# A recurrent step's tail re-ordered: which logarithm goes first on ScalarE, and where the 1e-10 term stands on VectorE

## The chip, the cores and the metric

The kernel runs on one core of a Trainium2 chip. The metric is the device time of one execution in microseconds; lower is better. The time of the kernel before is the median of three runs.

## What is computed

The reference is a network of eight sublayers on an input of 2 x 2048 x 256. The change lies in the first sublayer only, a recurrence over the 2048 positions ("the scan"). Its state h is a complex number for each of 2 batches, 256 channels and 16 modes. Cut to what matters, one position does this:

```
def step(h, inp):
    x_t, dt_t, B_t, C_t, xr_t = inp
    h_carrier = h.mean(axis=1)                        # over the 256 channels
    T = cos((c_phase(xr_t) - c_phase(h_carrier)) / 2) ** 2
    alpha = exp(dt_t[..., None] * A_neg)
    expo = 1 + (1 - alpha) * 0.5 * (1 - T[:, None, :])
    mag, ph = c_mag(h), c_phase(h)                    # c_mag = sqrt(re^2 + im^2 + 1e-8)
    cmag = minimum(exp(expo * log(mag + 1e-8)), 10)   # c_phase = arctan2(im, re + 1e-10)
    h = from_polar(cmag, ph) + B_t * (dt_t * x_t)
    h = from_polar(tanh(c_mag(h)), c_phase(h))
    y_t = einsum('bnc,bdnc->bd', C_t, h)
    return h, y_t
```

So each position needs the one before it: a power of the magnitude, an added drive, then a tanh of the new magnitude at unchanged phase.

## The kernel before

Before the scan, `scan_tables` computes the tables that it reads and puts them into DRAM. After it come an output product and the other seven sublayers. The scan keeps the state on 128 partitions (2 batches x 16 modes x 4 groups of channels) with 64 channels in the free dimension, real and imaginary part apart, so nearly every operation of a step is one instruction on a 128 x 64 tile of fp32.

The loop over the positions has four rounds of 512 positions. Inside a round everything is written out: 32 groups of 16 positions, and within a group `step(k, ...)` for each position. Inside a round the program keeps the order in which the instructions are written (`tc.manual_schedule()`), each engine working through its own queue in that order; semaphore waits are derived from the data. Where an instruction has to wait for two engines, an event-semaphore instruction for the first wait stands ahead of it.

A step uses three engines, in this order of data:

- TensorE (line 407) turns the sums of the last state, `hs`, into the mean over the channels, `hc` and `hd`. ScalarE makes the inverse of its magnitude out of it (`sq` on line 415, `ln`, `ci`), VectorE a product with the normalised input (`dot`).
- VectorE multiplies the carried logarithm `lg` by the decay (`gl`, line 411), subtracts it from the carried `kd` (`ex`, line 421) and makes `ngd` from `gl` and `dot` (line 422). ScalarE makes the two factors `ea` (line 426) and `fac` (line 436) with Exp. VectorE multiplies the state by them and adds the drive `bx` (lines 433 to 441): `p`, the new state before the tanh.
- VectorE squares and adds: `m2` (line 448), the squared magnitude, and `r1` (line 450).
- The tail: ScalarE makes out of `m2` and `r1`, in a run of Ln and Exp, all that the tanh and the next step's logarithm need. `lm` is log m2, `m` the magnitude, `ir` the inverse of the radius, `e` = exp(-2m), `rm` the inverse of m^2, `le` = log(1 + e), `ld` = log(1 - e), `sg` = 1/(1 + e), `lb` = log(m2 + 1e-8), `k1` and `k2c` two small corrections. tanh m is (1 - e) sg.
- VectorE scales `p` by `ir` (line 472) and by e - 1 (line 474). Line 477 makes `dl`, the correction for the 1e-10 of the phase. Line 479 multiplies by `sg`, writes the new state into `hist` and its sum over the 64 channels into `hs`; each of the two is a custom instruction with a read of the accumulator behind it. Lines 483 to 486 make `th` = ld - le, `kc`, and from them the `lg` and `kd` of the next step.

`lm`, `m` and `lr` are tiles in PSUM (`le` reuses the tile `m`, `lb` the tile `lr`), each in a pool with one buffer for each name; the others lie in SBUF with two buffers each. In between, `act_gap` gives ScalarE the next step's drive and some work for the next group, and `dve_gap` gives VectorE a little work in some steps.

Of the kernel before, what the change touches and what calls it, by code (L numbers as in the profile page):

```python
# [17 lines left out]
AF = mybir.ActivationFunctionType  # L18
ALU = mybir.AluOpType
# [18 lines left out]
SMALL = 1e-10  # L38
MAG_EPS = 1e-8
# [20 lines left out]
def new(pool, shape, name, **kw):  # L60
    return pool.tile(list(shape), F32, name=name, tag=name, **kw)


class Kernel:
# [189 lines left out]
    def scan(self, y, dtd, dxd, tabd):  # L254
# [7 lines left out]
        V, A, G = nc.vector, nc.scalar, nc.gpsimd  # L262
        J, TURN = 64, TG * GROUPS
        with ExitStack() as c:
# [129 lines left out]
            w = lambda sh, name: new(wp, [P, *sh], name)  # L394
            wa = lambda name: new(pa, [P, J], name)

            def step(k, g, before, act_gap, dve_gap):

                tc_, ng, dx, cs = tg[g]
                ng = ng[:, k]  # L400
                h = hist[g][:, k - 1] if k else hist[1 - g][:, TG - 1]
                hn = hist[g][:, k]
                i, o = (k + 1) % 2, k % 2

                for out in (hc, hd):
                    for r in range(0, P, 32):
                        nc.tensor.matmul(out[r : r + 32], mean[:, r : r + 32], hs[i], start=True, stop=True)  # L407
                before()

                gl, ex, ea, ngd = (w([J], n) for n in ("gl", "ex", "ea", "ngd"))  # L410
                V.tensor_tensor(gl, lg[i], ng, ALU.mult)


                sq, n2c = w([2], "sq"), w([1], "n2c")
                A.activation(sq, hc, AF.Square, accum_out=n2c)  # L415
                junk, dot = w([2], "junk"), w([1], "dot")
                V.tensor_tensor_reduce(
                    out=junk, in0=hd, in1=tc_[:, 4:6, k], scale=1.0, scalar=0.0, op0=ALU.mult, op1=ALU.add,
                    accum_out=dot,
                )  # L420
                V.tensor_tensor(ex, kd[i], gl, ALU.subtract)  # L421
                V.tensor_scalar(ngd, gl, dot, None, ALU.mult)
                ln, ci = wa("lr")[:, 0:1], w([1], "ci")
                A.activation(ln, n2c, AF.Ln, bias=1e-18)
                A.activation(ci, ln, AF.Exp, scale=-0.5)  # L425
                A.activation(ea, ex, AF.Exp)  # L426


                nc.tensor.matmul(hd[32:33, 0:1], ci, self.ident[:, 0:1], start=True, stop=True)  # L429


                p = w([2, J], "p")
                V.scalar_tensor_tensor(p[:, 0], h[:, 0], SMALL, ea, ALU.add, ALU.mult)  # L433
                V.tensor_tensor(p[:, 1], h[:, 1], ea, ALU.mult)  # L434
                fac = w([J], "fac")
                A.activation(fac, ngd, AF.Exp, scale=ci)  # L436
                act_gap(k)
                for k2 in range(2):
                    V.tensor_tensor(p[:, k2], p[:, k2], fac, ALU.mult)  # L439
                for k2 in range(2):  # L440
                    V.tensor_tensor(p[:, k2], p[:, k2], bx[o][:, k2], ALU.add)  # L441
                z = w([J], "z")
                V.scalar_tensor_tensor(z, p[:, 0], -2.0 * SMALL, p[:, 0], ALU.add, ALU.mult)
                q = w([2, J], "q")
                V.tensor_tensor(q[:, 1], p[:, 1], p[:, 1], ALU.mult)
                V.tensor_tensor(q[:, 0], p[:, 0], p[:, 0], ALU.mult)
                m2 = w([J], "m2")
                V.scalar_tensor_tensor(m2, z, MAG_EPS, q[:, 1], ALU.add, ALU.add)  # L448
                r1 = w([J], "r1")
                V.scalar_tensor_tensor(r1, q[:, 0], 1e-19, q[:, 1], ALU.max, ALU.add)  # L450
                dve_gap(k)

                lm, m, lr = wa("lm"), wa("m"), wa("lr")
                A.activation(lm, m2, AF.Ln)  # L456
                A.activation(lr, r1, AF.Ln)
                A.activation(m, lm, AF.Exp, scale=0.5)
                ir, e, sg, rm, ld = (w([J], n) for n in ("ir", "e", "sg", "rm", "ld"))
                A.activation(ir, lr, AF.Exp, scale=-0.5)  # L460
                A.activation(e, m, AF.Exp, scale=-2.0)
                A.activation(rm, lm, AF.Exp, scale=-1.0)
                le = wa("m")
                A.activation(le, e, AF.Ln, bias=1.0)
                A.activation(ld, e, AF.Ln, scale=-1.0, bias=1.0)
                A.activation(sg, le, AF.Exp, scale=-1.0)  # L466
                lb, k1, k2c = wa("lr"), w([J], "k1"), w([J], "k2c")
                A.activation(lb, m2, AF.Ln, bias=MAG_EPS)
                A.activation(k1, rm, AF.Ln, scale=MAG_EPS, bias=1.0)
                A.activation(k2c, lb, AF.Exp, scale=-0.5)  # L470
                for k2 in range(2):
                    V.tensor_tensor(p[:, k2], p[:, k2], ir, ALU.mult)  # L472
                for k2 in range(2):
                    V.scalar_tensor_tensor(p[:, k2], e, -1.0, p[:, k2], ALU.add, ALU.mult)  # L474
                th, kc, dl = (w([J], n) for n in ("th", "kc", "dl"))

                V.scalar_tensor_tensor(dl, p[:, 0], 0.5 * SMALL, rm, ALU.mult, ALU.mult)
                for k2 in range(2):
                    V.tensor_tensor_reduce(  # L479
                        out=hn[:, k2], in0=p[:, k2], in1=sg, scale=-1.0, scalar=0.0 if k2 else J * SMALL,  # L480
                        op0=ALU.mult, op1=ALU.add, accum_out=hs[o][:, k2 : k2 + 1],
                    )
                V.tensor_tensor(th, ld, le, ALU.subtract)
                V.scalar_tensor_tensor(kc, k2c, 2.0 * MAG_EPS, k1, ALU.mult, ALU.add)
                V.scalar_tensor_tensor(lg[o], th, 2.0, kc, ALU.mult, ALU.add)
                V.scalar_tensor_tensor(kd[o], kc, 0.5, dl, ALU.mult, ALU.add)

# [23 lines left out]
            with tc.For_i(0, S, TURN) as iv:  # L511
                A.preload_act_table_set(LOG_EXP)
                with tc.manual_schedule():
                    late = None
                    for g in range(GROUPS):
# [4 lines left out]
                        def act_gap(k):  # L520
                            for k2 in range(2):
                                if k + 1 < TG:
                                    drive(j, k + 1, k2, (k + 1) % 2)
                                else:
                                    drive(nxt, 0, k2, 0)
                            if k == 1:
                                rows(iv + (g + 1) * TG, nxt)
                            if 3 <= k < 11:
                                decay(nxt, (k - 3) // 2 * 4, 4, (k - 3) % 2)

                        def dve_gap(k):
                            if k == 1 and late is not None:
                                outputs(*late)
                            if k in (3, 4):
                                picked(nxt, k - 3)

                        for k in range(TG):
                            def before():
                                if k:
                                    project(j, k - 1, yps)  # L540
                                elif late is not None:
                                    project(1 - j, TG - 1, late[1])

                            step(k, j, before, act_gap, dve_gap)
# [1151 lines left out]
```

## Time and profile before

| | us |
|---|---|
| median of 3 runs | 14359.62 (14356.21 to 14366.0) |
| the profiled execution, its own time | 14346.1 |
| its span | 14344.4 |
| span up to the first step, 0 to 365 | 365 |
| the scan, 365 to 10164 | 9799; VectorE busy 8279, ScalarE 7244, TensorE 2275 |
| all that follows, 10164 to 14344.4 | 4180; VectorE busy 1789, ScalarE 1176, TensorE 3382 |

The scan takes two thirds of the span. In it none of the engines is busy all the time. An instruction's time in the profile is a start and a duration; two instructions of one engine can overlap in it, because the next starts before the end of the one ahead is reported. Times in the timeline count from the start of the span.

### The profile page before, as it was taken

The page shows a single profiled execution, that of the slowest core. Times are in us where ns is not written, and L with a number is a line of the kernel's source. Part 1 is how long each engine was busy: PE and PEld are TensorE (multiplying, and loading weights), DVE is VectorE, ACT ScalarE, POOL GpSimd, SP SyncE. Part 2 cuts the span into 40 slices and gives each one's busy share as a digit, 9 for nine tenths or more (in the row PEclk, how much of TensorE's full clock was granted, in tenths as well). Part 3 has the DMA queues.
Part 4 walks back from the last instruction along what each step waited for, and adds up shares of the span by engine and source line. Part 5 has one row for each costly group of instructions (what it writes and reads, how often), then busy time and mean ns, then how long its engine had stood idle before and what let it go on. Part 6 is the DMA issues. An engine that isn't in the chain of part 4 may idle for free. (4 is left out here: it accounts for less than half of the span.)

```text
span 14344.4 us, 281730 instructions
## 1 busy us (share of the span) xinstructions
PE 5813.5 (41%) x76520; PEld 3906.4 (27%) x76520; DVE 10318.8 (72%) x65163; ACT 8541.6 (60%) x44786; POOL 419.1 (3%) x496
## 2 busy tenths in 40 slices
PE   4222222222222222222222222222698566978889
PEld 2111111111111111111111111111355444544445
DVE  6888888888888888888888888888576211455552
ACT  3777777777777777777777777777354000134442
POOL 0000000000000000000000000000000000121110
PEclk6555555555555555555555555555598788989999
DMA  3000000000000000000000000000000777132210
GB/s 78 13 16 15 15 16 16 14 16 16 14 16 16 13 17 16 13 16 16 13 16 17 13 16 16 16 14 16 13 4 21 170 182 173 40 77 35 34 28 14
DMA packets 349084, 461.07 MB, mean 32 GB/s; under 512 B 204930, under 2 KB 244937, under 8 KB 346452
## 3 DMA queue, kind: packets, MB, share of 16 engines
q1 hardware_dynamic: 296276, 319.90, 9.9%
q10 hardware_dynamic: 36352, 88.61, 2.6%
q0 software_dynamic: 14848, 34.36, 0.9%
q8 instruction: 612, 10.03, 0.3%
q14 instruction: 996, 8.16, 0.2%
HBM read 385.55 MB, written 52.46 MB: 31 GB/s over the span
## 5 line engine op out<-in xcount | busy, mean ns | idle before, releaser
L407 PE MATMUL hc<-hs,mean 128*32 128x2 f32 x16384 | 586.9, 203 | 7227.7 <-DVE hs L479 7164.0
L407 PEld LDWEIGHTS hc<-hs,mean 128*32 128x32 f32 x16384 | 411.1, 140 | 7441.1 <-DVE hs L479 7376.8
L472 DVE TENSOR_TENSOR p<-p,ir 128x64 f32<-128x64 f32 x4096 | 738.2, 221 | 1064.6 <-ACT ir L460 1064.6
L491 PE MATMUL yps<-cs,hist 128*64 128x8 f32 x8192 | 1225.0, 259 | 13.3 <-DVE hs L479 13.3
L456 ACT ACTIVATE lm<-m 128x64 f32<-128x64 f32 x2048 | 466.2, 228 | 1209.8 <-DVE m L448 1209.8
L388 ACT ACTIVATE bx<-dx,tc 128x64 f32<-128x64 f32 x4098 | 1169.5, 332 | 0.1
L1520 ACT ACTIVATE d_p<-ps_e 128x512 f32<-128x512 f32 (+3 forms) x1280 | 599.5, 537 | 757.5 <-PE ps_o L1501 532.0
L491 PEld LDWEIGHTS yps<-cs,hist 128*64 128x64 f32 x8192 | 1033.2, 218 | 45.4 <-DVE hs L479 13.8
L415 ACT ACTIVATE sq<-hc 128x2 f32<-128x2 f32 x2048 | 352.6, 172 | 1162.5 <-PE hc L407 1162.5
L479 DVE CUSTOM_DVE_ANT_0 hist<-p,sg 128x64 f32<-128x64 f32 x4096 | 746.6, 219 | 11.9 <-DVE hs L479 6.1
L474 DVE SCALAR_TENSOR_TENSOR p<-e,p 128x64 f32<-128x64 f32 x4096 | 738.3, 222 | 9.9 <-ACT sg L466 9.2
L439 DVE TENSOR_TENSOR p<-p,fac 128x64 f32<-128x64 f32 x4096 | 738.2, 221 | 8.9 <-DVE p L434 6.5
L441 DVE TENSOR_TENSOR p<-p,bx 128x64 f32<-128x64 f32 x4096 | 724.3, 218 | 2.6
L436 ACT ACTIVATE fac<-ngd,ci 128x64 f32<-128x64 f32 x2048 | 711.7, 348 | 1.0 <-DVE p L433 1.0
L433 DVE SCALAR_TENSOR_TENSOR p<-hist,ea 128x64 f32<-128x64 f32 x2048 | 459.8, 225 | 322.5 <-ACT ea L426 322.5
L1513 PE MATMUL ps_e<-d_qt,d_kt 128*128 128x512 f32 (+3 forms) x1280 | 557.1, 444 | 44.4 <-ACT d_p L1520 35.9
L407 PE MATMUL hd<-hs,mean 128*32 128x2 f32 x16384 | 544.9, 193 | 0.0
L426 ACT ACTIVATE ea<-ex 128x64 f32<-128x64 f32 x2048 | 524.3, 256 | 29.3 <-DVE ex L421 5.3
L1167 PE MATMUL ps_c<-toep,c_x 64*32 64x128 f32 x18432 | 384.4, 320 | 386.1 <-issue 384.8
L1470 PE MATMUL ps_m<-d_kt,d_qt 128*128 128x512 f32 (+3 forms) x1280 | 500.0, 437 | 99.5 <-DVE d_part L1475 39.7
L429 PE MATMUL hd<-ident,ci 128*1 128x1 f32 x4096 | 387.9, 164 | 353.2 <-ACT ci L425 345.7
L1480 DVE TENSOR_REDUCE d_part<-ps_m 128x1 f32<-128x512 f32 x768 | 494.9, 683 | 41.1 <-PE ps_m L1470 40.4
(441 smaller groups left out, 22085.9 us busy)
## 6 DMA issues: line engine op xcount, KB each, us to landing
toep<-in_C_krev ACTq DMA_DIRECT2D x64, 1216.0 KB, 14.5
toep<-in_C_krev SPq DMA_DIRECT2D x64, 1216.0 KB, 9.7
ng<-dtd SPq DMA_DIRECT2D x258, 256.0 KB, 3.5
dx<-dxd SPq DMA_DIRECT2D x258, 256.0 KB, 3.9
d_kt<-d_kd SPq DMA_DIRECT2D x128, 128.0 KB, 4.4
d_qt<-d_qd SPq DMA_DIRECT2D x128, 128.0 KB, 4.2
y<-ys SPq DMA_DIRECT2D x512, 8.0 KB, 1.9
c_xd<-c_xs POOLq DMA_DIRECT2D x32, 256.0 KB, 6.4
```

What stands on the lines that cost most here:

```text
L388: A.activation(bx[o][:, k2], tg[j][2][:, k], AF.Identity, scale=tg[j][0][:, k2, k : k + 1], bias=0.0 if k2 else SMALL,)
L407: nc.tensor.matmul(out[r : r + 32], mean[:, r : r + 32], hs[i], start=True, stop=True)
L426: A.activation(ea, ex, AF.Exp)
L436: A.activation(fac, ngd, AF.Exp, scale=ci)
L439: V.tensor_tensor(p[:, k2], p[:, k2], fac, ALU.mult)
L441: V.tensor_tensor(p[:, k2], p[:, k2], bx[o][:, k2], ALU.add)
L472: V.tensor_tensor(p[:, k2], p[:, k2], ir, ALU.mult)
L474: V.scalar_tensor_tensor(p[:, k2], e, -1.0, p[:, k2], ALU.add, ALU.mult)
L479: V.tensor_tensor_reduce(out=hn[:, k2], in0=p[:, k2], in1=sg, scale=-1.0, scalar=0.0 if k2 else J * SMALL, op0=ALU.mult, op1=ALU.add, accu ...
L491: nc.tensor.matmul(yps[:, k, :], hist[g][:, k, k2], tg[g][3][:, k2, k], start=k2 == 0, stop=k2 == 1)
L1513: nc.tensor.matmul(s[:, q0:], ks[kt // 4][:, hh, kt % 4 * P : (kt % 4 + 1) * P], q[:, hh, q0:], start=True, stop=not diag,)
L1520: A.activation(pr[:, q0:], s[:, q0:], AF.Exp, scale=0.25)
```

## The change

Both queues of the tail are re-ordered; the operations stay the same.

On ScalarE, behind `e`: before, rm, le, ld, sg, lb, k1, k2c; after, lb, le, sg, rm, k2c, ld, k1. `lb` gets a PSUM tile of its own name instead of taking over the tile of `lr`.

On VectorE, `dl` moves from ahead of the two reductions that write `hist` and `hs` to behind `kc`. It is made from the new state `hn` instead of from `p`: hn is -p sg, so with the factor -1e-10 instead of 0.5 x 1e-10 it has sg where it had 1/2. The two agree for a small magnitude, where e is near 1 and sg near 1/2.

```diff
                 A.activation(e, m, AF.Exp, scale=-2.0)
-                A.activation(rm, lm, AF.Exp, scale=-1.0)
+                lb, k1, k2c = wa("lb"), w([J], "k1"), w([J], "k2c")
+                A.activation(lb, m2, AF.Ln, bias=MAG_EPS)
                 le = wa("m")
                 A.activation(le, e, AF.Ln, bias=1.0)
+                A.activation(sg, le, AF.Exp, scale=-1.0)
+                A.activation(rm, lm, AF.Exp, scale=-1.0)
+                A.activation(k2c, lb, AF.Exp, scale=-0.5)
                 A.activation(ld, e, AF.Ln, scale=-1.0, bias=1.0)
-                A.activation(sg, le, AF.Exp, scale=-1.0)
-                lb, k1, k2c = wa("lr"), w([J], "k1"), w([J], "k2c")
-                A.activation(lb, m2, AF.Ln, bias=MAG_EPS)
                 A.activation(k1, rm, AF.Ln, scale=MAG_EPS, bias=1.0)
-                A.activation(k2c, lb, AF.Exp, scale=-0.5)
...
                 th, kc, dl = (w([J], n) for n in ("th", "kc", "dl"))
-
-                V.scalar_tensor_tensor(dl, p[:, 0], 0.5 * SMALL, rm, ALU.mult, ALU.mult)
                 for k2 in range(2):
                     V.tensor_tensor_reduce(
                         out=hn[:, k2], in0=p[:, k2], in1=sg, scale=-1.0, scalar=0.0 if k2 else J * SMALL,
...
                 V.tensor_tensor(th, ld, le, ALU.subtract)
                 V.scalar_tensor_tensor(kc, k2c, 2.0 * MAG_EPS, k1, ALU.mult, ALU.add)
+                V.scalar_tensor_tensor(dl, hn[:, 0], -SMALL, rm, ALU.mult, ALU.mult)
                 V.scalar_tensor_tensor(lg[o], th, 2.0, kc, ALU.mult, ALU.add)
                 V.scalar_tensor_tensor(kd[o], kc, 0.5, dl, ALU.mult, ALU.add)
```

## The prediction

> **What bounds the kernel now.** I first read the busy shares, then the stretches of the span, then the scan's waits, then the timeline of one step. The page's engine line shows no full engine:
>
> ```profile
> PE 5813.5 (41%) x76520; PEld 3906.4 (27%) x76520; DVE 10318.8 (72%) x65163; ACT 8541.6 (60%) x44786; POOL 419.1 (3%) x496
> ```
>
> The scan runs one step after another, 2048 times. The answer for line 411, the first VectorE instruction of a step, dates them:
>
> ```profile
> L411 DVE TENSOR_TENSOR gl<-lg,ng x2048: 215/218/226, 364.8 to 10158.8; 128x64 f32<-128x64 f32 x187
> ```
>
> (10158.8 - 364.8) / 2047 = 4.785 us a step, 9.8 ms of the 14.34 ms span. So the question is the latency of one step. The waits of the scan (from 1000 to 10000 us) show who is late:
>
> ```profile
> ACT lm L456 <- DVE m L448: 1110.0, 1881, 1.1
> ACT sq L415 <- PE hc L407: 1067.5, 1878, 0.9
> DVE p L472 <- ACT ir L460: 978.3, 1882, 0.6
> ```
>
> VectorE and ScalarE wait for each other once a step in turn: a chain of latencies. The tail of one step, and the head of the next, in the timeline (start, duration, engine, line, result):
>
> ```profile
> 4003.77 0.22 ACT L461 ACTIVATE e<-m 128x64 f32<-128x64 f32 x1
> 4003.88 0.22 ACT L462 ACTIVATE rm<-lm 128x64 f32<-128x64 f32 x1
> 4004.01 0.23 ACT L464 ACTIVATE m<-e 128x64 f32<-128x64 f32 x1
> 4004.18 0.24 ACT L465 ACTIVATE ld<-e 128x64 f32<-128x64 f32 x1
> 4004.23 0.36 DVE L474 SCALAR_TENSOR_TENSOR p<-e,p 128x64 f32<-128x64 f32 x2
> 4004.32 0.20 ACT L466 ACTIVATE sg<-m 128x64 f32<-128x64 f32 x1
> 4004.43 0.22 ACT L468 ACTIVATE lr<-m 128x64 f32<-128x64 f32 x1
> 4004.56 0.23 DVE L477 SCALAR_TENSOR_TENSOR dl<-p,rm 128x64 f32<-128x64 f32 x1
> 4004.57 0.24 ACT L469 ACTIVATE k<-rm 128x64 f32<-128x64 f32 x1
> 4004.70 0.22 DVE L479 CUSTOM_DVE_ANT_0 hist<-p,sg 128x64 f32<-128x64 f32 x1
> 4004.72 0.21 ACT L470 ACTIVATE k2c<-lr 128x64 f32<-128x64 f32 x1
> 4004.99 0.21 DVE L483 TENSOR_TENSOR th<-ld,m 128x64 f32<-128x64 f32 x1
> 4005.12 0.21 DVE L484 SCALAR_TENSOR_TENSOR kc<-k2c,k 128x64 f32<-128x64 f32 x1
> 4005.37 0.22 DVE L485 SCALAR_TENSOR_TENSOR lg<-th,kc 128x64 f32<-128x64 f32 x1
> ...
> 4005.52 0.22 DVE L486 SCALAR_TENSOR_TENSOR kd<-kc,dl 128x64 f32<-128x64 f32 x1
> ...
> 4005.65 0.22 DVE L411 TENSOR_TENSOR gl<-lg,ng 128x64 f32<-128x64 f32 x1
> ...
> 4006.16 0.26 ACT L426 ACTIVATE ea<-ex 128x64 f32<-128x64 f32 x1
> 4006.39 0.35 ACT L436 ACTIVATE fac<-ngd,ci 128x64 f32<-128x64 f32 x1
> ```
>
> ("m<-e" on 464 is le; "lr<-m" on 468 is lb.) From the stamps I take **slots** and **hand-overs**. A slot, start to next start, is shorter than a duration. VectorE's is 0.135 us; it is 0.19 (line 474's pair lasts 0.36, so its second starts at 4.37; dl follows at 4.56) where an instruction waits for two engines and the trace shows an event-semaphore instruction ahead of it. ScalarE's is 0.11 after an Exp (e to rm, sg to lb) and 0.14 to 0.17 after a Ln (lb to k1 0.14, le to ld 0.17). A dependent instruction starts 0.03 to 0.04 after its producer's end (kc ends 5.34, lg starts 5.37; ScalarE's ir to VectorE's line 472 also 0.04).
>
> The tail is set by VectorE's queue: the pair of 474, dl, the reductions of 479, th, kc; then by results, kc to lg to gl to ex and ngd to ea and fac. All Ln and Exp of the tail are ready when asked for: k2c ends at 4004.93, kc starts at 5.12. The mean path (hs, matmul, sq, ci) isn't binding: by the same timeline ci ends at 4006.15, while fac starts at 6.39 because ngd (started 6.05, 0.25 long) ends at 6.30.
>
> **What the Trainium skill says.** "Perfetto Trace Analysis", DVE / Act Engine Instruction, has the end stamp include the write's acknowledgement and the next instruction begin earlier: slots shorter than durations, as here (0.135 against 0.22). Its Identifying Dependency Chains says that waits on several engines may put an EventSemaphore ahead; here 21 ns of it precede each of the 2048 dl. "ScalarE: Activation LUTs", What ACT_TABLE_LOAD costs, has all functions cost the same; the durations agree (0.20 to 0.24) but the slots here don't quite, Ln taking 0.03 more than Exp, and I use the slots. Its section on table sets has exp and ln in one set; line 512's 4 table loads in the scan agree, so no reordering of Ln and Exp adds loads.
>
> **The change, part by part.** Nothing is added or removed: 12 activations (456 to 470) and 11 VectorE operations (472 to 486) before and after. lb gets a PSUM tile of its own. No DMA, GpSimd or SP work moves. I place the same step's instructions anew; e stays at 3.77 (all ahead of it is untouched).
>
> *lb in rm's slot.* lb starts at 3.88; its slot of 0.14 puts le at 4.02, where le waited for e until 4.01: +0.01, covered by e's own latency.
>
> *sg right behind le.* le ends at 4.25 (0.23), sg starts at 4.29 instead of 4.32, ends at 4.49. VectorE sees it at 4.53.
>
> *dl behind the sums.* The first reduction takes dl's place behind line 474. It now waits for two engines (p and sg), so it inherits dl's 0.19: 4.56 instead of 4.70, **0.14 earlier**; sg is there with 0.03 to spare. Behind it are the second reduction, 4.70, and th, free at 4.85. hs is 0.14 earlier, so the matmul and sq too; ci then ends about 0.2 or more ahead of need, so that is worth nothing by itself.
>
> *ld and k1 last.* Behind sg (4.29): rm 4.40, k2c 4.51, ld 4.62, k1 4.76 to 4.78 (a Ln slot). ld ends at 4.86, so th starts at 4.90: **a new wait** of 0.05 at th, in front of kc, dl, lg, kd and gl. k1 ends (0.24) at 5.00 to 5.02, so kc starts at 5.04 to 5.06 (th + 0.135 gives 5.03). Against 5.12: 0.06 to 0.08 earlier. Of the 0.14 about half goes into ScalarE's new lateness.
>
> *dl between kc and lg.* There VectorE was idle: kc to lg is 0.25, one slot is 0.135. With dl the slots make 0.27: **+0.02**. lg starts at 5.31 to 5.33; kd, which now also waits for dl (start kc + 0.135, end kc + 0.36), at lg + 0.15, no later than before; gl at lg + 0.28, 5.59 to 5.61 instead of 5.65.
>
> The sum is 0.04 to 0.06 a step by these rounded stamps. Means over some 77 undisturbed steps give e 2.855, le to sg 0.266, four Exp slots of 0.105 to 0.115 and two Ln slots of 0.145 to 0.165, thus kc at 4.127 to 4.145 after gl instead of 4.215, and, less 0.02, 0.05 to 0.07. I take **0.06**: 2048 x 0.06 = 123 us. The profiled execution's own time is 14346.1 (span 14344.4 and 1.7 around it); 14346.1 - 123 = 14223. It stands 13.5 under the median of the runs shown, 14359.62; 14359.6 - 123 = 14237.
>
> **Unknown costs.** (a) A reduction with an event semaphore ahead is not in the trace. Nearest are dl's 0.19 and the custom operation's own 0.14; I take 0.19. The slack is 0.05, because th waits for ld anyway; at +0.10 it would cost 0.05 a step. At 0.14 it gains nothing, as sg isn't there sooner. (b) Exp behind Exp with both reading PSUM (rm, k2c) is seen once, m to ir at 0.10, Ln behind Exp at 0.11; bounds 0.10 and 0.14, so -0.03 to +0.09 over three slots; I take 0.11. (c) ld to k1: 0.14 to 0.17; taken 0.15. (d) Some steps last 0.3 longer (the mean of 4.785 against a usual 4.74); I leave these pauses alone, and allow 0.01 a step either way.
>
> **Rivals.** *ScalarE doesn't hold th and kc back* (k1 done 0.05 sooner): the reductions' 0.14 less dl's 0.02 remain, 0.12 a step, 246 us: 14114. For it: today every one of these results is early. Against: ld is now eleventh of the tail's twelve in ScalarE's queue instead of eighth, and k1 is the last. Chance 0.06.
>
> *The gain is eaten exactly:* k1 0.06 later than reckoned (Ln slots of 0.17 and an Exp slot or two at 0.14) puts lg back at 5.37: 14360. Chance 0.05.
>
> *ScalarE's tail becomes the bound, and a longer one:* slower. Place: k1, whose end frees kc. If the three slots behind sg and the one behind ld are those of a Ln that the trace shows at its longest, 0.17, that is 3 x 0.06 + 0.02 = 0.20 later, less the 0.06: 0.14 a step, +287 us, 14647; half of it, 0.10, gives 0.04, +82 us, 14442. It decides from k1's end at 5.08 on. For it: in the new order two waits (le for e, sg for le) stand back to back with no independent work between. Against: sg also follows a wait today and lb is issued 0.11 behind. Chance 0.06.
>
> That the order isn't the written one is no rival: in the built program both queues stand as in the diff, and lg waits for kc, not for dl.
>
> **How the numbers follow.** About 0.2% (29 us, 0.014 a step) is what a measurement can tell from no change. Forecast 0.83, the three rivals 0.06, 0.05 and 0.06. Faster is the forecast and the first rival, 0.89, plus a share of the second: 0.90; same 0.04; slower 0.06. The range takes (a) to (d) in part: gains of 0.024 to 0.095 a step, 50 to 195 us, so 14165 to 14310.
>
> **What would show it.** In the profile after: the reductions directly behind line 474; th with a small wait for ld (0.03 to 0.07, some 60 to 140 us in all) that before doesn't have; kc right at the end of k1; dl in the gap between kc and lg with lg 0.27 behind kc; a step of about 4.68 in the usual case. sq should start about 0.08 earlier before gl than now. It is wrong if sg makes the first reduction wait, if k1 ends 0.06 or more later than reckoned, or if lg waits for dl.

## The result and the profile after

The changed kernel takes 14232.39 us (median of 4 runs, 14220.57 to 14246.55) against 14357.92 before: a ratio of 0.9912 with a 95% interval of 0.9895 to 0.9929, or 125.5 us less. The prediction was 14237, in the range 14165 to 14310. The profiled execution of the changed kernel took 14220.57 us with a span of 14218.9, so it lies at the low end of its runs.

The page's engine line, and the answer for line 411, which dates the steps:

```profile
PE 5816.9 (41%) x76520; PEld 3913.9 (28%) x76520; DVE 10262.3 (72%) x65163; ACT 8647.8 (61%) x44786; POOL 418.9 (3%) x496
```

```profile
L411 DVE TENSOR_TENSOR gl<-lg,ng x2048: 216/219/226, 365.5 to 10042.3; 128x64 f32<-128x64 f32 x187
```

The number of instructions is the same on every engine; VectorE is 57 us less busy, ScalarE 106 us more, with the same activations. From the first to the last step it is 9676.8 us instead of 9794.0. Dating all 2047 intervals between the steps' first instructions in both traces splits the 117.2 us:

| | before | after | difference, us |
|---|---|---|---|
| a step without a pause, mean, us | 4.7445 | 4.6893 | -0.0552 x 2047 = -113.0 |
| steps longer than that by 0.06 to 2: number, what they add | 236, 63.1 us | 230, 59.2 us | -3.9 |
| the three turns of the loop of rounds | 18.9 us | 18.7 us | -0.2 |

The spans differ by 125.5; the remaining 8.3 us lie outside the scan, where nothing was changed, and compare one execution with one. In the nine traces of this document the part outside the scan took 4527 to 4550 us, so 8.3 us there say nothing about the change.

The same part of a step in the timeline of the changed kernel (start, duration, engine, line, result; "m<-e" is le, "k<-rm" is k1, and the line numbers from 463 on have moved):

```profile
4008.91 0.22 ACT L461 ACTIVATE e<-m 128x64 f32<-128x64 f32 x1
4009.02 0.23 ACT L463 ACTIVATE lb<-m 128x64 f32<-128x64 f32 x1
...
4009.16 0.22 ACT L465 ACTIVATE m<-e 128x64 f32<-128x64 f32 x1
4009.37 0.36 DVE L474 SCALAR_TENSOR_TENSOR p<-e,p 128x64 f32<-128x64 f32 x2
4009.41 0.22 ACT L466 ACTIVATE sg<-m 128x64 f32<-128x64 f32 x1
4009.53 0.22 ACT L467 ACTIVATE rm<-lm 128x64 f32<-128x64 f32 x1
4009.64 0.23 ACT L468 ACTIVATE k2c<-lb 128x64 f32<-128x64 f32 x1
4009.74 0.23 DVE L477 CUSTOM_DVE_ANT_0 hist<-p,sg 128x64 f32<-128x64 f32 x1
4009.74 0.27 ACT L469 ACTIVATE ld<-e 128x64 f32<-128x64 f32 x1
4009.89 0.27 ACT L470 ACTIVATE k<-rm 128x64 f32<-128x64 f32 x1
...
4010.04 0.22 DVE L481 TENSOR_TENSOR th<-ld,m 128x64 f32<-128x64 f32 x1
...
4010.19 0.22 DVE L482 SCALAR_TENSOR_TENSOR kc<-k2c,k 128x64 f32<-128x64 f32 x1
...
4010.33 0.22 DVE L483 SCALAR_TENSOR_TENSOR dl<-hist,rm 128x64 f32<-128x64 f32 x1
4010.46 0.22 DVE L484 SCALAR_TENSOR_TENSOR lg<-th,kc 128x64 f32<-128x64 f32 x1
...
4010.73 0.22 DVE L411 TENSOR_TENSOR gl<-lg,ng 128x64 f32<-128x64 f32 x1
```

From e to the next gl it is 1.82 us here; before it was 1.88 (4003.77 to 4005.65). The reduction (line 477) follows the pair of 474. th starts 0.03 after ld's end (4010.01), and kc starts 0.03 after k1's end (4010.16): VectorE and ScalarE finish the tail together. dl stands in the gap between kc and lg, which is 0.27 now.

### The profile page after: what moved, and what is told of

It reads as the page before. It is cut to its first block, busy times and chain, and to the rows that moved or that the text cites. A ratio compares the mean times of both kernels' runs of the same rounds, so it can differ in the third digit from the quotient of the medians.

```text
span 14218.9 us, 281730 instructions
## 1 busy us (share of the span) xinstructions
PE 5816.9 (41%) x76520; PEld 3913.9 (28%) x76520; DVE 10262.3 (72%) x65163; ACT 8647.8 (61%) x44786; POOL 418.9 (3%) x496
## 5 line engine op out<-in xcount | busy, mean ns | idle before, releaser
L469 ACT ACTIVATE ld<-e 128x64 f32<-128x64 f32 x2048 | 548.0, 268 | 0.0
L470 ACT ACTIVATE k<-rm 128x64 f32<-128x64 f32 x2048 | 545.9, 267 | 0.0
```

## The experiments

All times below are from one chip, on which the kernel before took 14339.86 us (first four kernels) and 14338.52 us (last three), 9 runs each. The first four expectations were reckoned from the 14358 us of the result above, so some 18 us of their distance to the measured times are the chip's. Step times and places are means over undisturbed steps of each trace, and a place "after gl" counts from the start of the step's first VectorE instruction.

### Only the VectorE part: dl behind kc, ScalarE as before

```diff
-                V.scalar_tensor_tensor(dl, p[:, 0], 0.5 * SMALL, rm, ALU.mult, ALU.mult)
...
                 V.scalar_tensor_tensor(kc, k2c, 2.0 * MAG_EPS, k1, ALU.mult, ALU.add)
+                V.scalar_tensor_tensor(dl, hn[:, 0], -SMALL, rm, ALU.mult, ALU.mult)
```

> Only the VectorE part of the change (dl behind kc); ScalarE's order as before. Theory: dl's place gives the whole gain, and sg need not come earlier: the first reduction is held by its two waits behind line 474 (0.23 after the second of the pair in the changed kernel, while sg had ended 0.10 before), and th and kc find all of ScalarE's results ready (k2c ends 4.02 after gl). Then th starts at 4.00 after gl, kc at 4.13, lg at 4.41, the step is 4.68 to 4.69, and the time is 14215 to 14245, equal to the changed kernel's 14232. Rival: the earlier sg is what lets the first reduction go early; with sg ending at 3.61 instead of 3.59 and the reduction 0.10 behind it, the reduction starts at 3.72, the step is 4.71 and the time about 14290. Second rival: ScalarE's order brings the gain; then this kernel is within 0.2% of 14358.

Measured: 14174.14 us, ratio 0.9885 (0.9870 to 0.9900). This is faster than was expected, and faster than the whole change. In the timeline:

```profile
4007.39 0.36 DVE L474 SCALAR_TENSOR_TENSOR p<-e,p 128x64 f32<-128x64 f32 x2
4007.49 0.20 ACT L466 ACTIVATE sg<-m 128x64 f32<-128x64 f32 x1
...
4007.76 0.23 DVE L478 CUSTOM_DVE_ANT_0 hist<-p,sg 128x64 f32<-128x64 f32 x1
4007.88 0.21 ACT L470 ACTIVATE k2c<-lr 128x64 f32<-128x64 f32 x1
...
4008.06 0.22 DVE L482 TENSOR_TENSOR th<-ld,m 128x64 f32<-128x64 f32 x1
4008.19 0.22 DVE L483 SCALAR_TENSOR_TENSOR kc<-k2c,k 128x64 f32<-128x64 f32 x1
```

The reduction starts 0.37 behind the start of line 474, as in the changed kernel (4009.37 to 4009.74). By the means it starts at 3.69 after gl in both, though sg ends at 3.622 here and at 3.594 there. So sg's new place didn't bring the reduction forward; the first rival is out, and with the gain itself the second. The step is 4.667, a little under the expected 4.68: th starts at 3.992 and kc at 4.125, free of ScalarE, whose last result k2c ends at 4.025, and lg follows kc by 0.271. In the changed kernel kc starts at 4.141, because k1 ends at 4.109. The whole gain comes from dl's move, and the new ScalarE order takes some of it back.

### Only the ScalarE part: dl stays ahead of the reductions

The edit is the ScalarE half of the diff above.

> Only the ScalarE part of the change; dl stays ahead of the reductions. Theory: slower. dl needs rm, which now ends at 3.71 after gl instead of 3.19; dl starts at 3.75 instead of 3.65, and all behind it on VectorE is 0.10 later: a step of 4.84, + 205 us, about 14560. Rival: the ScalarE order is worth something alone (sg 0.04 earlier), 14275 to 14358.

Measured: 14507.47 us, ratio 1.0116 (1.0100 to 1.0131): slower.

```profile
4009.71 0.22 ACT L466 ACTIVATE sg<-m 128x64 f32<-128x64 f32 x1
4009.83 0.22 ACT L467 ACTIVATE rm<-lm 128x64 f32<-128x64 f32 x1
...
4010.08 0.23 DVE L476 SCALAR_TENSOR_TENSOR dl<-p,rm 128x64 f32<-128x64 f32 x1
...
4010.22 0.22 DVE L478 CUSTOM_DVE_ANT_0 hist<-p,sg 128x64 f32<-128x64 f32 x1
```

rm ends at 4010.05 and dl starts 0.03 later; the reduction, whose sg is done at 4009.93, stands behind dl in the queue and has to wait for it. The step is 4.834, 0.089 over the kernel before, or 183 us over 2047 steps; the 168 us measured are a little less because the pauses add 49.5 us here instead of 63.1. The two halves of the change aren't two separate gains: the ScalarE half is a loss alone, and is bearable only because dl no longer needs rm early.

### The changed kernel without dl

```diff
-                V.scalar_tensor_tensor(dl, hn[:, 0], -SMALL, rm, ALU.mult, ALU.mult)
...
-                V.scalar_tensor_tensor(kd[o], kc, 0.5, dl, ALU.mult, ALU.add)
+                V.tensor_scalar(kd[o], kc, 0.5, None, ALU.mult)
```

> The changed kernel with dl left out (kd = 0.5 kc; the 1e-10 correction of the phase is not computed). Theory: dl lies almost wholly in the gap between kc and lg, so only 0.02 to 0.03 a step goes: kc to lg 0.25 instead of 0.28, 40 to 60 us under the changed kernel, 14170 to 14195. Rival: dl costs its slot of 0.135 on the chain behind kc as it did ahead of the reductions; then 277 us less, about 13955.

Measured: 14161.40 us, ratio 0.9877 (0.9862 to 0.9892). kc to lg is 0.259 instead of 0.278, the step 4.669 instead of 4.689: dl costs 0.02 of its 0.135 slot where it now stands, 41 us over 2047 steps. (kd is another instruction here, 0.19 long instead of 0.22; the step's 0.02 include that.) The changed kernel takes 14225 on this chip, 64 us more: some 40 are the steps and 6 the pauses. The rest can lie outside the scan, which took 4527 us in this trace, the least of the nine. The rival (dl's whole slot on the chain) would have been 277 us and is out.

### th ahead of the reductions, with ScalarE's old order

The VectorE part alone leaves VectorE idle between the pair of line 474 and the reduction. Here th fills that place:

```diff
                 th, kc, dl = (w([J], n) for n in ("th", "kc", "dl"))
+                V.tensor_tensor(th, ld, le, ALU.subtract)
...
-                V.tensor_tensor(th, ld, le, ALU.subtract)
                 V.scalar_tensor_tensor(kc, k2c, 2.0 * MAG_EPS, k1, ALU.mult, ALU.add)
+                V.scalar_tensor_tensor(dl, hn[:, 0], -SMALL, rm, ALU.mult, ALU.mult)
```

> ScalarE's order as before, dl behind kc as in the changed kernel, and th ahead of the two reductions. Theory: VectorE is idle for about 0.10 between the pair of line 474 and the first reduction, because that waits for p and then for sg; th fits in there (ld ends 3.51 after gl, th starts at 3.60), the reductions start at 3.74 to 3.79, and kc, with th gone from in front of it, at about 4.05 (held by k2c's end at 4.02) to 4.08. lg follows at 4.33 to 4.36, the step is 4.60 to 4.63, and the time 14105 to 14175, 60 to 125 us under the changed kernel. The sums hs come 0.05 to 0.09 later than in the changed kernel, which costs nothing if the mean path has the slack that I read. Rival: the idle time is not free (the reduction's own two waits cost 0.19 to 0.23 behind th again), or the mean path binds; then th's move gains nothing and the time is 14225 or more.

Measured: 14057.06 us, ratio 0.9802 (0.9789 to 0.9816), 283 us under the kernel before: the fastest version here, and under the expected range, though the step lies in the expected 4.60 to 4.63.

```profile
4006.04 0.24 ACT L465 ACTIVATE ld<-e 128x64 f32<-128x64 f32 x1
4006.09 0.36 DVE L474 SCALAR_TENSOR_TENSOR p<-e,p 128x64 f32<-128x64 f32 x2
4006.18 0.20 ACT L466 ACTIVATE sg<-m 128x64 f32<-128x64 f32 x1
...
4006.42 0.22 DVE L476 TENSOR_TENSOR th<-ld,m 128x64 f32<-128x64 f32 x1
...
4006.56 0.22 DVE L479 CUSTOM_DVE_ANT_0 hist<-p,sg 128x64 f32<-128x64 f32 x1
...
4006.85 0.22 DVE L483 SCALAR_TENSOR_TENSOR kc<-k2c,k 128x64 f32<-128x64 f32 x1
```

The reduction starts at 3.791 after gl, only 0.096 later than without th in front, and kc at 4.081, so the step is 4.625. th starts 0.04 after sg's end (4006.38), not after ld's (4006.28), and by the means 0.032 after sg's end: its wait for ScalarE is one for sg, which serves the reduction behind it too. Where VectorE had paused and sg was done early, th follows the pair by 0.135 or 0.14. The reduction has a single wait left and follows th by an ordinary slot, 0.14. The event semaphore, which in the changed kernel stands ahead of it in every step, as the answer for line 477 there has it, is gone from the trace:

```profile
L477 DVEq EVENT_SEMAPHORE  x2048: 21/21/21, 370.5 to 10045.9; - x187
```

Of the 283 us, 0.1195 x 2047 = 245 are shorter regular steps. Another 34 are pauses: 112 steps have one instead of 236, and they add 29.2 us instead of 63.1 (more on them in the last section).

hs comes 0.09 later here than in the changed kernel (the second accumulator read ends at 4.163 after gl instead of 4.074) while the step is shorter. So the mean path had the slack that the prediction gave it. It is nearly used up: ci now ends at 0.620 after gl, and ngd, which fac waits for as well, at 0.643.

### th ahead of the reductions, with ScalarE's new order

The same move of th, made in the changed kernel.

> th ahead of the reductions, as in e4_th_first, but with ScalarE's order of the changed kernel (ld ninth-last to late: its end at 3.97 after gl instead of 3.52). Theory: the place of th fits only the old ScalarE order. th, and behind it the whole VectorE queue, waits for ld until 4.01 instead of 3.67; reductions 4.14 and 4.29, kc 4.43, lg 4.71, a step of 4.98, 0.29 over the changed kernel and 0.24 over the kernel before: about 14820. Rival: the new order costs only its 0.02 a step here too, about 14105.

Measured: 14759.62 us, ratio 1.0295 (1.0279 to 1.0311). What line 476 (th) waited for, in the answer for that line:

```profile
its engine sat idle before it (us, times) until:
  ACT ld L469: 634.4, 2016
```

634.4 / 2016 = 0.31 us a step. This counts from the reported end of the instruction ahead; from start to start th is 0.34 later than with the old order, at 3.995 after gl instead of 3.652, and the step of 4.967 is 0.34 longer. In the changed kernel the late ld was hidden, since th stood behind two reductions; move th and it is all exposed. The total is 60 us under the expected 14820: the pauses add 20 us here instead of 63.1, and the step is 0.013 shorter than reckoned.

### The VectorE part and the whole change, side by side

> e1_dve_only once more, beside the changed kernel on one chip. Theory: the new ScalarE order costs the changed kernel 0.023 a step (4.689 against 4.667), so this kernel is 40 to 55 us faster than the changed kernel. Rival: the two are equal within 15 us, and the difference between the two earlier comparisons was the chip's.

> The changed kernel once more, on the same chip as the two others. Theory: 40 to 55 us over the kernel with only the VectorE part, and 110 to 130 us under the kernel before. Rival: equal to the kernel with only the VectorE part within 15 us.

Measured on one chip: 14168.80 us, ratio 0.9883 (0.9868 to 0.9899), and 14225.16 us, ratio 0.9917 (0.9904 to 0.9931). The VectorE part alone is 56 us faster than the whole change, a little more than was expected. In these two traces a regular step takes 4.6607 and 4.6879: 0.0272 x 2047 = 56 us. In the first traces of the two kernels it was 4.6665 and 4.6892, or 46 us, so a step's mean can differ by 0.006 between two executions of one kernel.

## Why the prediction was right

Its sum was 0.06 a step and 123 us; 0.0552 a step and 125.5 us were measured. Only 113 of the 125.5 us are what it reckoned with; the rest are pauses and the part outside the scan, so that the totals lie so close is in part luck. Side by side on the chip of the experiments the gain was 113.4 us (14338.52 to 14225.16). By its own steps, after gl:

| | before | predicted | after |
|---|---|---|---|
| sg starts | 3.413 | 0.03 earlier | 3.371 |
| first reduction starts | 3.793 | 0.14 earlier (3.65) | 3.694 |
| th starts | 4.083 | 0.09 earlier, after a wait of 0.05 for ld | 3.997 |
| k1 ends | 3.906 | 0.19 to 0.21 later | 4.109 |
| kc starts | 4.215 | 4.127 to 4.145 | 4.141 |
| kc to lg | 0.251 | + 0.02 | 0.278 |
| a step | 4.7445 | 0.06 less | 4.6893 |

*lb in rm's slot, sg behind le:* as predicted, to about 0.01. That sg mattered was implied by the order of the argument and is not so; the VectorE part alone does without it.

*dl behind the sums:* the mechanism was right, the size of its first term was not. The first reduction came 0.099 earlier, not 0.14. The mis-sized term is unknown cost (a): behind line 474 the reduction with an event semaphore ahead of it starts 0.23 after the second of the pair, where I took dl's 0.19. sg isn't the cause, as shown above; and where VectorE paused ahead of the pair, so that sg was done before the pair's second began, the distance is still 0.22 or 0.23 in 28 of 32 steps. Neither the custom operation nor the event semaphore makes it alone: an ordinary operation starts 0.135 behind the one ahead without an event semaphore and 0.19 with it (dl before), the reduction 0.14 without (th first) and 0.23 with it. Why the event semaphore costs the reduction more was not tried.

*ld and k1 last:* the step that carries the number. kc starts at 4.141, inside the predicted 4.127 to 4.145, 0.03 behind k1. Inside so narrow a range it fell partly by luck: k1 lasts 0.024 longer than the old 0.243, which the prediction used, and sg starts 0.25 behind le's start instead of the 0.266 that it used. (The range has only the last slot's spread; with the shortest or the longest of its slots throughout, its sum runs from about 4.11 to 4.19.) The predicted sign, a visible wait of th for ld of 60 to 140 us in all, is not in the trace. The answer for line 481 of the changed kernel has only this:

```profile
its engine sat idle before it (us, times) until:
  ACT k L470: 0.7, 4
```

The sign was ill chosen: the answer counts idle time only from the reported end of the instruction ahead, and the second reduction's end, 4.066 after gl, lies behind th's start, so a wait of 0.05 would not have shown there either. From start to start th follows the second reduction by 0.153 instead of 0.146, so it waits under 0.01. The reason is the late reduction: it used up 0.044 of the 0.05 that th would have waited (th is free at about 3.99, ld is there at 4.00). The prediction had named this slack under its cost (a), so the late reduction costs nothing by its own mechanism: ScalarE's k1 sets kc's start, and the terms 0.14 less 0.06 for ScalarE's lateness came out as 0.10 less 0.02. By the same stamps a reduction at 3.65 would have left the step as it is, and one later than about 3.70 would have lengthened it; that was not run.

*dl between kc and lg:* + 0.02 predicted, + 0.027 measured, and 0.02 by leaving dl out.

*hs earlier is worth nothing:* shown by the kernel with th first, where hs is later and the step shorter. The expected sign, sq about 0.08 earlier before gl, came out at 0.03 (sq stood 0.172 ahead of the next gl and stands 0.204 ahead now), as the reductions gained less.

*Rivals:* ScalarE's tail did become a bound in the changed kernel, but not one that makes the step longer than before. The slots were as taken: 0.12, 0.10 and 0.10 from sg to ld, and 0.15 from ld to k1; none was near the 0.17 that would have made it slower. What was longer are ld and k1 themselves, 0.27 each instead of 0.24. k1's end, which decides, came at 4.109, about 0.06 before the point (4.215 less 0.02 for dl and 0.03 for the hand-over, about 4.17) from which the gain would have been gone. The first rival, ScalarE not holding th and kc back, is not the changed kernel but is the VectorE part alone: it was priced at 0.14 less 0.02, 0.12 a step, and is 0.078 there, 0.10 less 0.02.

## What to carry to other kernels

In a chain that two engines hand back and forth, an operation whose result is wanted late belongs in a gap in which its engine waits for a result anyway: dl cost 0.10 us ahead of the sums and 0.02 behind kc, and th in the gap in front of the reduction brought another 0.04 us a step. Before a producer's queue is re-ordered so that one result comes earlier, look whether the consumer was waiting for that result; here it wasn't, and the order only made the last results later (46 to 56 us of the gain given back). Changes of two queues belong together where one engine's order fixes when the other's operands come: the same ScalarE order costs 0.02 us a step with dl and th late, 0.09 with dl early and 0.34 with th early (4.967 against 4.625).

## What the runs showed of the hardware

The same activation does not take the same time in every place of ScalarE's queue: with the new order ld and k1 take 0.27 us instead of 0.24, lb and k2c 0.23 instead of 0.22 and 0.21, sg 0.22 instead of 0.20. le takes 0.22 instead of 0.23. Busy time counts overlaps once, so these lengths don't add up to the 106 us by which ScalarE is busier with unchanged work; its unbroken run from lm to the last result of the tail lasts 1.77 us instead of 1.69.

An event semaphore ahead of a VectorE instruction lengthened the distance from start to start: for dl 0.19 instead of an ordinary 0.135, for the reduction 0.23 instead of 0.14.

Some steps have a pause of 0.06 to 0.4 us on VectorE that no wait explains, and the first step of each round one of 1.2 to 1.5 us: 236 steps before (63 us), 230 after, 201 without dl (53 us), 112 with th first, 66 with th first and ScalarE's new order. They are not scattered. 58 of a round's 512 steps pause in all four rounds of the kernel before, and 57 of these 58 do so in the changed kernel. Count the VectorE instructions of a round in the trace, event semaphores included, with the round's first gl as number 0. Then in all nine traces each paused step, but for one step of each round (the 93rd), holds an instruction with a number of 16 more than a multiple of 128. The reverse does not hold: in the kernel before 520 steps hold such an instruction and 232 of them pause. The kernel without dl and the two with th first have one VectorE instruction fewer in a step, so these numbers fall on other instructions, and they pause in other steps: all 27 that pause in every round with th first are among the 49 without dl. With th first and ScalarE's old order, none of the pauses at these numbers falls on the reductions or behind them in the tail; without dl 104 do, the event semaphore ahead of the reductions included. What the engine does at these numbers stays open.
